# Sparse graph attention on one core: every operation gets a place of its own in its engine's order

## The chip, the cores and the metric

The kernel runs on one NeuronCore of one Trainium2 chip. The metric is the device time of one execution in microseconds (us), measured over several runs; the median is compared. TensorE (PE in the profile), VectorE (DVE), ScalarE (ACT), GpSimd (POOL) and SyncE (SP) each work through a queue of their own, in the order in which the program emits their instructions, and wait for each other by semaphores. SP issues plain transfers; POOL issues the indirect ones (gathers and scatters by a list of row numbers).

## What is computed

One layer of graph attention with a residual, for 16 batches of 1024 nodes with 512 features, 8 heads of 64, all in float32. The adjacency matrix is sparse and shared by all batches; its diagonal is set.

```
h = maximum(layernorm(x), 0)                       # no scale, no offset
q, k, v = h @ Wq + bq, h @ Wk + bk, h @ Wv + bv    # (16, 1024, 8, 64)
scores = einsum('bihd,bjhd->bhij', q, k) / sqrt(64)
scores = scores + where(adj == 0, -1e9, 0)
out = einsum('bhij,bjhd->bihd', softmax(scores), v)
return x + out
```

## The kernel before

**The work.** A score matters only where adj is not 0, so the kernel gathers each node's neighbours and computes nothing dense. It does so in two stages.

The *head* (some 100 us, once) finds the neighbours. SP loads the adjacency as eight tiles of 128 rows (`load_adj`, L664). DVE counts each row's entries (`degree`, L709 and L713), POOL clears the diagonal (`no_diagonal`, L718), `keys` (L724) makes sort keys, TensorE turns them into rows (`flip_row`, L735), and DVE and ACT rank the nodes by comparing (`rank_of`, L745 and L749; `ranks`). Nodes are sorted by degree, so that each tile of 128 nodes needs its own small number of neighbour slots, `CAPS = (11, 8, 6, 5, 4, 3, 3, 2)`. Lists of neighbours are made (`list_of`, L906), scattered to tables in DRAM by POOL (`tell`, `spread`, L910), collected by SP (`collect`, L922), and turned into gather indices (`spots`, `long_rows`, `long_blocks`, `longest`, `pieces`, `slots`). Rows with more than 10 neighbours are cut into *pieces* of 4 that stand in a tile of their own.

The head also projects keys and values of batch 0. Its x tiles are loaded by SP (`load_x`, L786), normed and projected like those of every later batch.

The *batches*: DVE makes the statistics of an x tile (`stats`, `variance`, `shift` L813) with a power on POOL (`power`, L809); ACT norms it (`norm`, L823); TensorE transposes it (`flip`, L830), ACT copies it back (`unflip`, L835), TensorE multiplies it with Wk and Wv (`proj_kv`, L843), ACT or DVE takes the result out of PSUM (`evict_kv`, L861 and L859), and SP stores it as rows of k|v (`store_kv`, L885; in batch 0 POOL by a scatter, L881). The attention of one batch runs beside the projections of the next. It goes by 14 *units*, each of 2 to 4 neighbour slots of one tile: `queries` (TensorE), `gather` (POOL by index, L1093; a node's own row by SP, L1091), `multiply` (L1103) and `score` (L1107) on DVE, `exponent` (ACT, L1111), the weighing of v (`weigh_s` on ACT, L1129, eight small activations each; `weigh_v` on DVE, L1123), sums of the slots (`fold` L1134 on DVE or POOL, `join` L1141, or `add_up` on TensorE, L1157), division by the softmax sum (`scale`, L1198), residual (L1207) and output (`put_out`, L1210, a scatter by POOL). The pieces' unit of tile 0 takes its queries from tile 0's: ACT copies them to SBUF (`copy_q`, L1074), and TensorE spreads them to the pieces with a matmul by the matrix `owner` (L1070); `pass_on` (L1177) returns the pieces' softmax sums.

**The bias.** It is added in PSUM by a matmul of a row of ones (`chosen`) with three bf16 parts of the bias (`project`, L841; `add_bias`, L847, for the very first tile). The parts are made once: `load_b` (L682) loads the three vectors into rows of one tile `rest`, and `round` (ACT, L698 and L700) and `remain` (POOL, L703) take turns on it:

```
def round(j):
    if j < 2:
        nc.scalar.activation(part, rest, AF.Identity, scale=later[j])
    else:
        nc.scalar.copy(bias, rest)
def remain(j):
    nc.gpsimd.tensor_tensor(rest, rest, part, ALU.subtract)
```

**What sets the order.** `planned` (from L265) lists every operation with its engine, what it must follow, which buffers of which pool it uses, and a *place*: a number computed from the batch, the tile or unit, one offset for each kind of operation (`AT`, L73) and some single corrections (`FINE`, L83). `Plan.ordered` (L179 to L257) then plays the program through with a cost for each kind (`LENGTHS`, L106): whenever an engine is free, it takes the operation with the lowest place among those whose inputs are done and whose buffers are free. The sequence that comes out is the order in which the operations are emitted, and so each engine's queue. An operation that is not ready in this play-through is passed by others.

Transfers issued by SP use eight semaphores in turn, so each waits until the eighth before it has landed.

Of the kernel before, what the change touches and what calls it, by code (L numbers as in the profile page):

```python
# [32 lines left out]
P = 128  # L33
H = 8
# [26 lines left out]
LAST_TILES = (0, 1, 2, 3, 4, 5, 6, 7)  # L61
LAST_ORDER = tuple(UNITS.index(unit) for t in LAST_TILES for unit in PARTS[t])
LAST_DIRECT = (7,)
POOL_FOLDS = ((5, 0), (4, 0), (1, 0), (1, 4), (-1, 0))
# [8 lines left out]
AT = dict(  # L73
    load_x=170.09, stats=-5.83, variance=-6.1, power=-47.58, shift=-11.83, norm=-65.99, flip=-3.5, unflip=-69.44, proj_kv=-0.17,
    evict_kv=-1.04, queries=-0.21, own=7.45, gather=-8.51, score=1.54, exponent=37.66, row_sums=-33.29, share=-103.18,
    weigh_v=-4.42, weigh_s=56.4, fold=-4.42, join=-3.58, add_up=-5.47, direct_residual=3.86, direct_out=-0, more=-116.77,
    pass_on=-0.94, sums=-5.02, scale=-1.48, residual=-38.62, put_out=-47.81, seen=11.6, zero=-5.59, zero_rate=0.56,
    ahead=-14.69, early=0.02, early2=0.33, early3=0.24, first=-60.83, first_rate=7.61, v_late=9.54, key_row=-221.51,
    rank_row=-80.11, rank_d=-9.75, rank_a=45.47, ranks=-75.78, ends=-96.51, list_of=76.9, tell=-79.58, spread=-44.68,
    others=-101.81, spots=-59.47, long_rows=-152.98, long_0=-64.75, long=-72.37, longest=20.9, count=-6.64, pieces=2.43,  # L80
    setup=-64.27, parts=-10.1, spread_bias=-5.47, copy_q=131.7, fetch_q=-35.12, evict_v=0.78, bias_v=-48.9,
)
FINE = {  # L83
    ('owners',): -1.5, ('rank_of', 0): 5.46, (-1, 'evict_kv', 7, 0): 0.78, (-1, 'proj_kv', 2, 1): 6.9,
    (-1, 'proj_kv', 6, 0): 9.56, (-1, 'proj_kv', 7, 0): 8.02, (0, 'multiply', 4): 10.01, (0, 'queries', 0, 1): -1.48,
    (0, 'queries', 0, 7): 5, (0, 'weigh_s', 5, 0): -10.62, (1, 'evict_kv', 3, 1): -0.64, (1, 'flip', 1): 0.71,
    (1, 'fold', 11, 1, 1): 0.79, (1, 'fold', 12, 2, 2): 2.15, (1, 'fold', 8, 1, 1): 1.26, (1, 'fold', 8, 2, 2): 2.12,
    (1, 'gather', 8, 3): 0.98, (1, 'join', 9): 3.14, (1, 'multiply', 5): 1.61, (1, 'multiply', 6): 1.34,
    (1, 'proj_kv', 0, 0): -0.95, (1, 'proj_kv', 2, 0): 1.26, (1, 'put_out', 0, 4): -1.57, (1, 'put_out', 0, 5): -2.25,
    (1, 'score', 13): -5.29, (1, 'score', 5): 3.73, (1, 'score', 9): -0.38, (1, 'shift', 1): 3.92, (1, 'weigh_s', 6, 1): 1.85,  # L90
    (1, 'weigh_v', 11): -2.61, (1, 'weigh_v', 9): -1.9, (2, 'add_up', 1): 3.15, (2, 'add_up', 3): 6.42,
    (2, 'evict_kv', 5, 1): 3.83, (2, 'gather', 12, 0): 1.34, (2, 'gather', 3, 1): -1.6, (2, 'gather', 4, 2): -1.63,
    (2, 'gather', 6, 2): -2.75, (2, 'gather', 7, 2): -2.05, (2, 'gather', 8, 3): -1.07, (2, 'gather', 9, 0): 2.03,
    (2, 'gather', 9, 1): 2.13, (2, 'proj_kv', 1, 1): 1.06, (2, 'proj_kv', 2, 1): 1.64, (2, 'proj_kv', 3, 0): 14.3,
    (2, 'proj_kv', 4, 1): -0.54, (2, 'proj_kv', 6, 0): -1.82, (2, 'residual', 0, 4): 2.64, (2, 'residual', 0, 6): 7.2,
    (2, 'score', 7): -2.13, (2, 'store_kv', 6): -3.35, (2, 'variance', 1): 1.8,
# [3 lines left out]
JOIN = False  # L100
BIAS_V = {0: 'DVE', 2: 'DVE', 4: 'DVE', 6: 'DVE'}
PAIRED = ()
FETCH = False


LENGTHS = dict(  # L106
    zeros=(0.15, 2.0, 0.0), load_w=(0.2, 2.5, 3.0), load_b=(0.6, 2.2, 0.0), load_adj=(0.2, 2.5, 1.5),
    spread_bias=(0.22, 0.2, 0), copy_bias=(0.47, 0.15, 0), bias_v=(1.43, 0.0, 0),
    setup=(1.0, 0.1, 0), add_bias=(0.22, 0.2, 0), join_acc=(0.602, 0.13, 0),
    parts_at=(0.4, 0.13, 0), warm=(1.3, 0.1, 0), round=(0.58, 0.15, 0), remain=(1.2, 0.1, 0), degree=(1.4, 0.13, 0), no_diagonal=(0.3, 0.1, 0),  # L110
    keys=(0.45, 0.13, 0), flip_row=(0.45, 0.2, 0), copy_row=(0.68, 0.13, 0), rank_of=(1.28, 0.13, 0), ranks=(1.1, 0.13, 0),
    ends=(1.1, 0.13, 0), list_of=(2.46, 0.13, 0), tell=(1.28, 2.5, 0), spread=(1.5, 2.5, 0), collect=(0.05, 2.6, 0),
    others=(1.25, 0.13, 0), perm_of=(0.4, 0.13, 0), spots=(4.0, 0.13, 0), long_rows=(1.25, 4.0, 1.5), long_blocks=(3.4, 0.13, 0),
    longest=(1.02, 0.13, 0), count_pieces=(0.8, 0.13, 0), first_piece=(0.45, 0.2, 0), owners=(0.95, 0.13, 0), flip_owners=(0.27, 0.2, 0),
    copy_owners=(0.25, 0.13, 0), list_pieces=(0.4, 0.2, 0), pieces=(1.0, 0.13, 0), slots=(1.6, 0.13, 0),
    load_x=(1.25, 3.0, 0.68), stats=(0.818, 0.13, 0), variance=(0.1, 0.13, 0), power=(1.2, 0.0, 0), shift=(0.08, 0.13, 0),
    norm=(0.719, 0.13, 0), flip=(0.437, 0.2, 0), unflip=(0.465, 0.15, 0), proj_kv=(3.649, 0.2, 0), evict_kv=(0.465, 0.15, 0),
    store_kv=(0.1, 2.6, 1.36), proj_q=(3.649, 0.2, 0), evict_q=(0.465, 0.15, 0), store_q=(0.1, 2.6, 0.68), fetch_q=(1.25, 3.0, 0.68),
    queries=(3.649, 0.2, 0), copy_q=(0.487, 0.15, 0), gather=(1.25, 3.0, 1.36), multiply=(0, 0.13, 0), score=(0, 0.13, 0),
    exponent=(0.125, 0.14, 0), row_sums=(0.371, 0.13, 0), share=(0.117, 0.13, 0), weigh_v=(0, 0.13, 0), weigh_s=(1.91, 0.14, 0),  # L120
    fold=(0, 0.13, 0), join=(0.602, 0.13, 0), add_up=(0.858, 0.2, 0), more=(0.133, 0.13, 0), pass_on=(0.14, 0.2, 0),
    scale=(0.602, 0.13, 0), residual=(0.602, 0.13, 0), put_out=(1.30, 3.0, 0.68), seen=(0.25, 0.13, 0),
)
LENGTHS["fold", "POOL"] = LENGTHS["residual", "POOL"] = (1.43, 0.0, 0)
LENGTHS["evict_kv", "DVE"] = (0.602, 0.13, 0)
LENGTHS["gather", "SP"] = (0.1, 3.0, 1.36)
LENGTHS["load_x", "SP"] = (0.2, 2.5, 0.75)
LENGTHS["store_kv", "POOL"] = (1.25, 2.6, 1.36)
PAIR = {1: 0.602, 2: 1.131, 3: 1.668, 4: 2.198}
SHARED = ("fold", "join", "bias_v",  "weigh_v", "residual", "scale", "power")  # L130


BY_UNIT = ("gather", "multiply", "score", "exponent", "weigh_v", "weigh_s", "fold", "join", "add_up", "share")
BY_TILE = ("load_x", "stats", "norm", "flip", "unflip", "proj_kv", "evict_kv", "store_kv", "bias_v")
BY_HOME = ("queries", "row_sums", "residual", "put_out", "scale", "more", "pass_on", "copy_q", "store_q", "fetch_q", "seen")


def spot_of(key, B):

    name, *rest = key
    if name in BY_UNIT:
        b, at = divmod(rest[0], NU)
    elif name in BY_TILE:
        b, at = divmod(rest[0], NT)
    elif name in ("variance", "power", "shift"):
        b, at = divmod(rest[0], NT // group_of(rest[0] * GROUP)[2])
    elif name in BY_HOME:
        b, at = rest[0], 0  # L150
    else:
        return (name, *rest)
    return (min(b, 1) + (b == B - 1), name, at, *rest[1:])


class Plan:

# [6 lines left out]
    def add(self, key, engine, place, after=(), uses=(), length=None, delay=None, moves=None):  # L170

        self.number[key] = len(self.ops)
        long, late, bytes_ = LENGTHS.get((key[0], engine)) or LENGTHS[key[0]]
        length = long if length is None else length
        delay = late if delay is None else delay
        place = place + FINE.get(spot_of(key, self.batches), 0.0)
        self.ops.append((key, engine, length, place, after, uses, delay, bytes_ if moves is None else moves))

    def ordered(self, bufs):  # L179
        ops = [op[:3] + (round(op[3], 4),) + op[4:] for op in self.ops]  # L180
        follow = [[] for _ in ops]
        missing = [len(op[4]) for op in ops]
        left, line = {}, {}
        for i, op in enumerate(ops):
            for key in op[4]:
                follow[self.number[key]].append(i)
        for op in sorted(ops, key=lambda op: op[3]):
            for use in op[5]:
                if use not in left:
                    left[use] = 0  # L190
                    line.setdefault(use[0], []).append(use)
                left[use] += 1
        given = {pool: 0 for pool in line}
        has = set()

        def can_start(op):
            for use in op[5]:
                if use not in has:
                    pool = use[0]
                    n = given[pool]  # L200
                    if line[pool][n] != use or (n >= bufs[pool] and left[line[pool][n - bufs[pool]]]):
                        return False
# [1206 lines left out]
```

## Time and profile before

| what | value |
| --- | --- |
| timed runs | 1636.62, 1629.81 and 1636.53 us, median 1636.53 us |
| profiled execution | 1644.55 us, span 1642.9 us |
| mean granted TensorE clock | 0.989 of full speed |
| instructions | 19494 |
| DMA | 531.71 MB, 324 GB/s over the span |
| first multiply (L1103) of batch 0 | 108.58 us |
| last projection of K and V ends | 1534.0 us |

The profile is one execution, taken by the hardware profiler; its span is the time between its first and last instruction. The page lists the busy time of each engine with the number of instructions, then the span in slices. Other answers of the trace: the same busy times for any stretch (with the TensorE clock that was granted, the busy share of the DMA engines and their GB/s), the waits of an engine (what ended each, the sum, how many, the longest), and a timeline (start, length, engine, line, output <- input, shape, how many instructions in a row, and in brackets the idle time before them with what ended it). A name with q at the end, as SPq, is that engine's issuing of transfers. Two TensorE records belong to one float32 matmul of 128x512.

### The profile page before, as it was taken

What the parts mean: (1) busy time and instruction counts of PE and PEld (TensorE: products, weight loads), DVE (VectorE), ACT (ScalarE), POOL (GpSimd) and SP (SyncE); (2) the same over time, 40 slices, a digit from 0 to 9 for tenths busy, and PEclk for the clock granted to TensorE, in tenths of its full rate; (3) what the DMA queues carried; (4) which work ended last, traced back from release to release, by engine and by line L of the source; (5) the groups of instructions that cost most, each with busy time, mean ns of one, the idle gap of its engine ahead of it and who ended that gap; (6) DMA issues with size and microseconds to landing.
All of it is one profiled execution on the core that took longest, in us unless ns stands there. A gap on an engine that the chain in (4) does not pass through costs nothing. (4 is left out here: it accounts for less than half of the span.)

```text
span 1642.9 us, 19494 instructions
## 1 busy us (share of the span) xinstructions
PE 1574.6 (96%) x4236; PEld 729.9 (44%) x4236; DVE 1525.6 (93%) x2081; ACT 1444.9 (88%) x5420; POOL 1248.7 (76%) x1184
## 2 busy tenths in 40 slices
PE   6899999999999999999999999999999999999696
PEld 3454444444444444444444444444444444444232
DVE  7779999999999999999999999999999999999996
ACT  4258989998998989899898999989999998999885
POOL 3766878778878877887878877888787778777764
PEclk9999999999999999999999999999999999999898
DMA  6487989989899998989999998999989899998993
GB/s 246 138 313 242 360 328 338 362 318 365 313 347 329 355 355 318 358 318 349 336 331 365 327 370 302 337 337 348 352 322 349 301 346 336 348 354 312 339 359 123
DMA packets 150740, 531.71 MB, mean 324 GB/s; under 512 B 19916, under 2 KB 19916, under 8 KB 150616
## 3 DMA queue, kind: packets, MB, share of 16 engines
q0 software_dynamic: 109840, 390.70, 66.6%
q1 hardware_dynamic: 40776, 139.71, 22.0%
q14 instruction: 89, 0.73, 0.1%
q8 instruction: 35, 0.57, 0.1%
HBM read 429.51 MB, written 100.82 MB: 323 GB/s over the span
## 5 line engine op out<-in xcount | busy, mean ns | idle before, releaser
L1129 ACT ACTIVATE g<-g,weights 128x64 f32<-128x64 f32 x4696 | 1154.4, 337 | 18.8 <-DVE weights L1116 10.8
L1093 POOL DMA_INDIRECT g<-kv,index x608 | 638.9, 1051 | 221.7 <-issue 176.4
L843 PE MATMUL pq<-wq,hT 128*128 128x512 f32 x1024 | 460.3, 592 | 0.0
L843 PE MATMUL pk<-wk,hT 128*128 128x512 f32 x960 | 432.9, 594 | 0.0
L843 PE MATMUL pv<-wv,hT 128*128 128x512 f32 x960 | 431.5, 592 | 0.1
L1107 DVE TENSOR_REDUCE weights<-g 128x32 f32<-128x2048 f32 (+2 forms) x224 | 422.5, 1888 | 0.7
L1103 DVE TENSOR_TENSOR g<-g,pq 128x1536 f32<-128x1536 f32 (+2 forms) x208 | 388.7, 1870 | 27.5 <-DMA g<-kv,index 11.3
L843 PEld LDWEIGHTS pq<-wq,hT 128*128 128x128 f32 x1024 | 194.6, 190 | 221.5 <-issue 217.8
L843 PEld LDWEIGHTS pk<-wk,hT 128*128 128x128 f32 x960 | 182.9, 191 | 216.9 <-issue 212.9
L843 PEld LDWEIGHTS pv<-wv,hT 128*128 128x128 f32 x960 | 180.1, 190 | 191.6 <-issue 187.6
L1134 DVE TENSOR_TENSOR g<-g 128x512 f32<-128x512 f32 (+1 forms) x301 | 253.5, 844 | 8.1 <-ACT g L1129 5.3
L1210 POOL DMA_INDIRECT out_dram<-x,perm x128 | 137.8, 1076 | 40.8 <-issue 18.9
L788 POOL DMA_INDIRECT x<-in_x_dram,perm x128 | 131.7, 1029 | 38.5 <-issue 37.6
L1134 POOL TENSOR_TENSOR g<-g 128x512 f32<-128x512 f32 x90 | 114.0, 1275 | 5.0 <-DVE g L1134 2.8
L1111 ACT ACTIVATE weights<-weights 128x32 f32<-128x32 f32 (+2 forms) x224 | 49.8, 223 | 77.2 <-DVE weights L1107 60.5
L1123 DVE TENSOR_TENSOR g<-g,weights 128x512 f32<-128x512 f32 x149 | 109.0, 739 | 2.9 <-ACT weights L1111 2.8
L1207 POOL TENSOR_TENSOR x<-x,o 128x512 f32<-128x512 f32 x67 | 86.1, 1285 | 17.8 <-DVE o L1198 14.9
L823 ACT ACTIVATE h<-x,shift,rstd 128x512 f32<-128x512 f32 x120 | 92.4, 806 | 0.5 <-DVE shift L813 0.5
L830 PEld LDWEIGHTS pht<-ident,h 128*128 128x128 f32 x512 | 64.3, 145 | 63.6 <-issue 54.2
L1157 PE MATMUL acc<-g,ident 128*128 128x512 f32 x170 | 83.9, 607 | 2.4 <-ACT g L1129 1.5
L835 ACT COPY hT<-pht 128x512 f32<-128x512 f32 x128 | 73.0, 575 | 14.9 <-PE pht L830 13.1
L797 DVE BATCH_NORM_STATS2 st<-x 128x6 f32<-128x512 f32 x120 | 81.5, 679 | 2.5 <-DMA x<-in_x_dram,perm 2.4
(242 smaller groups left out, 1108.3 us busy)
## 6 DMA issues: line engine op xcount, KB each, us to landing
g<-kv SPq DMA_DIRECT2D x128, 512.0 KB
kv<-kvt SPq DMA_DIRECT2D x120, 512.0 KB
g<-kv,index POOLq DMA_INDIRECT x608
adj<-in_adj_dram SPq DMA_DIRECT2D x8, 512.0 KB
x_first<-in_x_dram SPq DMA_DIRECT2D x8, 256.0 KB
x<-in_x_dram,perm POOLq DMA_INDIRECT x128
out_dram<-x,perm POOLq DMA_INDIRECT x128
wk<-in_L_gnn_Wk_dram SPq DMA_DIRECT2D x1, 1024.0 KB
```

The lines of the kernel that those rows point to most:

```text
L788: nc.gpsimd.indirect_dma_start(out=X[n][:], out_offset=None, in_=x_rows, in_offset=on(ap=perm[:, t : t + 1], axis=0), element_offset=b * N * D
L823: nc.scalar.activation(HN[n], X[n], AF.Relu, bias=shift, scale=scale)
L843: nc.tensor.matmul(pt, HT[n][:, c, :], W[name][:, c, :], start=(apart and c == 0), stop=(n != -NT and c == DC - 1))
L1093: nc.gpsimd.indirect_dma_start(out=G[i][:, s].rearrange("p j d -> p (j d)"), out_offset=None, in_=KV[b % len(KV)][:], in_offset=on(ap=inde ...
L1103: nc.vector.tensor_tensor(k, k, Q[b, t][:, None, :].to_broadcast([P, count, D]), ALU.mult)
L1107: nc.vector.tensor_reduce(weights[:, w, :], heads(G[i][:, :count, 0, :]), AX.X, ALU.add)
L1123: nc.vector.tensor_tensor(v, v, own.to_broadcast([P, n, H, HD]), ALU.mult)
L1129: nc.scalar.activation(v[:, h, :], v[:, h, :], AF.Identity, scale=weights[:, c + s, h : h + 1])
L1134: engine.tensor_tensor(v[:, 0:n], v[:, 0:n], v[:, first : first + n], ALU.add)
L1157: nc.tensor.matmul(ACC[b, home], owner_t if t < 0 else ident, v[:, s, :], start=(u == added_up(b, B, home)[0] and s == 0), stop=(u == adde ...
L1207: (nc.vector if residual_by_vector(b, B, t) else nc.gpsimd).tensor_tensor(rows, rows, add, ALU.add)
L1210: nc.gpsimd.indirect_dma_start(out=out_rows, out_offset=on(ap=perm[:, t : t + 1], axis=0), in_=X.pop(b * NT + TILES.index(t))[:], in_offse ...
```

## The change

The set of operations stays the same, but for three small matmuls that are added, a dependence that is replaced, and two tiny copies that vanish with a path that was switched off.

1. **Order.** The offsets, corrections, costs and the play-through go. In their place a table `PLACES` gives every operation a number of its own: one block for operations that happen once, one for the projections of batch 0 (`first`), one each for batches 0, 1 and 2, one for the batches 3 to 13, one for batch 14 (`next`) and one for batch 15 (`last`). A batch's numbers are moved by `PERIOD` for each batch. `ordered` sorts each engine's operations by this number alone, so an operation is never passed by another of its engine; the queues are merged so that everything is emitted behind what it needs.
2. **Dependences.** `round(0)` must now follow the second norm instead of the first power.
3. **TensorE warmed.** `warm_pe`: three float32 matmuls of 128x512 on the tile that the biases go into, their results unused. They are first in TensorE's queue.
4. **Last batch.** The order of its units is written out as a list: unit 6 now comes ahead of 9, and unit 3 ahead of 5.
5. **Dead code.** Fetching the pieces' queries from DRAM, joining the pieces on DVE, and a column of `found0` go, with two one-column copies of DVE (L998 and L1019). A multiplication on POOL (`weigh_p`) is added, but no unit uses it.

The diff, cut to its core (the other changes of `planned` take the place and the costs out of each `add`):

```diff
-AT = dict(
-    load_x=170.09, stats=-5.83, variance=-6.1, power=-47.58, shift=-11.83, norm=-65.99, flip=-3.5, unflip=-69.44, proj_kv=-0.17,
...
+PERIOD = 95.290021
+PLACES = {
+    'once': dict(
+        zeros=(9.38,),
+        load_w=(2.39, 6.93, 22.86,),
+        load_b=(13.19, 1.37, 6.73,),
+        load_adj=(1.87, 3.6, 4.6, 2.13, 3.77, -0.33, 3.93, 1.93,),
+        warm=(89.31,),
+        warm_pe=(3.75,),
+        setup=(-0.4, 0.06, 3.61,),
+        parts_at=(10.69,),
+        round=(4.36, 4.39, 6.59,),
+        remain=(2.93, 16.84,),
+        degree=(10.86, 14.18, 21.61, 11.08, 14.91, 10.62, 17.65, 12.88,),
...
+    'first': dict(
+        load_x=(94.59, 95.26, 95.84, 97.13, 101.65, 101.71, 104.87, 110.73,),
...
+        power=(95.83, 104.16, 131.48, 140.22,),
...
     def ordered(self):
+        place = self.places()
+        number = self.number
+        known = [[number[key] for key in op[2]] for op in self.ops]
+        waiting = {}
+        for i in sorted(range(len(self.ops)), key=place.__getitem__):
+            waiting.setdefault(self.ops[i][1], []).append(i)
...
+        while len(result) < len(self.ops):
+            ready = []
+            for engine, queue in waiting.items():
+                if head[engine] == len(queue):
                     continue
...
+                i = queue[head[engine]]
+                new = [use for use in self.ops[i][3] if use not in has]
+                if all(k in made for k in known[i]) and all(given[use[0]] == at[use] for use in new):
+                    ready.append((place[i], i, new))
+            _, i, new = min(ready)
...
+    add(("warm_pe",), "PE")
...
-        known = [("remain", j - 1)] if j else [("parts_at",), ("power", -NT // 2)] + [("load_b", name) for name in names]
-        add(("round", j), "ACT", AT["parts"] + j, known)
+        known = [("remain", j - 1)] if j else [("parts_at",), ("norm", 1 - NT)] + [("load_b", name) for name in names]
+        add(("round", j), "ACT", known)
...
-LAST_TILES = (0, 1, 2, 3, 4, 5, 6, 7)
-LAST_ORDER = tuple(UNITS.index(unit) for t in LAST_TILES for unit in PARTS[t])
+LAST_ORDER = (10, 11, 12, 13, 8, 6, 9, 7, 4, 3, 5, 2, 1, 0)
...
+        def warm_pe():
+            p = ps_a.tile([P, D], F32, tag="acc", name="p_warm")
+            for _ in range(3):
+                nc.tensor.matmul(p, ident, rest, start=True, stop=True)
```

(`first` numbers are lowered by one `PERIOD`, so they stand on the same scale as `once`; the three entries of `load_b` are those of k, v and q.)

## The prediction

> **What bounds the kernel now.** I read the page's busy line first, then the same sums by stretch, then TensorE's waits, then the timeline of the first 27 us. The busy line:
>
> ```profile
> span 1642.9 us, 19494 instructions
> ...
> PE 1574.6 (96%) x4236; PEld 729.9 (44%) x4236; DVE 1525.6 (93%) x2081; ACT 1444.9 (88%) x5420; POOL 1248.7 (76%) x1184
> ```
>
> TensorE leads, but a mean over stages does not say where it waits. By stretches (start:end, length, then busy us of each engine with its instructions, granted clock, DMA share, GB/s):
>
> ```profile
> 0.00:40.00 40.00, 26.65 (x84) 13.90 (x85) 29.67 (x83) 18.92 (x30) 14.12 (x35) 1.00 0.71 253
> ...
> 200.00:1440.00 1240.00, 1226.10 (x3302) 568.20 (x3301) 1180.42 (x1513) 1151.47 (x4368) 987.38 (x917) 1.00 0.93 339
> 1440.00:1534.00 94.00, 94.00 (x249) 43.14 (x247) 88.79 (x111) 86.79 (x334) 72.10 (x68) 1.00 0.93 344
> 1534.00:1605.00 71.00, 53.37 (x119) 22.21 (x118) 63.72 (x61) 63.70 (x267) 45.14 (x44) 0.88 0.92 337
> ```
>
> In the long middle TensorE idles 1240 - 1226.1 = 13.9 us and nobody else comes near; from 1534 on (no projections left) DVE and ACT lead, and the serial output transfers end the run. So a change of order can gain at most about 14 us in the middle, and something at the two ends. TensorE's own waits (us in all, times, longest):
>
> ```profile
> PE pht_first L830 <- ACT h_first L823: 11.2, 1, 11.2
> ...
> PE pht L830 <- ACT h L823: 6.2, 1, 6.2
> ...
> PE pq_-1_10415 L1070 <- ACT q L1074: 2.2, 1, 2.2
> PE p_key L735 <- DVE key L724: 1.7, 1, 1.7
> ```
>
> The third is the repeated one: the pieces' query (L1070) waits for ScalarE's copy of tile 0's query (L1074) in nearly every batch. The timeline of the middle gives these waits as .48, .06, .96, 1.13, .1, 1.05, .1, 1.22, .05, .9, 2.19, 1.33 and 1.39: 11.0 us together. Another 2.4 us are short waits for free PSUM at L841.
>
> **The head, +7 us (bounds 0 and +16).** Every operation of the first 100 us gets a new place. The one that matters is the load of the K bias. All three bias vectors (6 KB each, as three equal rows) go into one tile, which round(0) (L698) reads, and round(0) is now queued on ACT behind the second norm. Before, the three loads are SP's 4th to 6th transfers, issued at 2.19 to 2.95 us, and the round runs at 9.71:
>
> ```profile
> 9.71 0.72 ACT L698 ACTIVATE scratch<-scratch,later 128x512 bf16<-128x512 f32 x1 [7.22 <-DMA scratch<-in_L_gnn_bq_dram]
> ```
>
> After, SP's order is four x tiles with one adjacency tile and bv among them, three more adjacency tiles, wk (10th), the other four, two x tiles, bq (17th), wv (18th), the seven zero stores (19th to 25th), an x tile, and only then bk, the **27th**. SP issues a transfer only when the eighth before it has landed (the program's instruction list shows that wait on each). Before, its last transfers of the same stretch go out so:
>
> ```profile
> 20.95 3.21 SPq L676 DMA_DIRECT2D told<-scratch  x2
> 24.43 0.94 SPq L676 DMA_DIRECT2D lists<-scratch  x2
> 25.98 0.33 SPq L786 DMA_DIRECT2D x_first<-in_x_dram  x1
> ```
>
> The 25th is issued at about 25, the 27th at 25.98. After, as many bytes lie ahead, so bk is issued at about 25.5 and lands at about 27.5 (25.5 to 29).
>
> What queues behind: on POOL remain(0) stands fourth, ahead of one setup and of power for the second pair of tiles; behind that power stands DVE's shift, and behind the shift five of the eight degrees (L709, L713) and the keys. From the rows: round 0.72, remain 1.16 with a start of 0.05, setup 0.7, power 0.73, shift 0.2: DVE is free at 31.1. Five degrees at 1.35 make 37.9, the keys 0.46: 38.3, where TensorE now gets them here:
>
> ```profile
> 24.25 1.09 PE L735 MATMUL p_key<-ident,key 128*128 128x128 f32 x8 [1.69 <-DVE key L724]
> ```
>
> That is 14 us later. TensorE meanwhile: three warming matmuls as soon as bv is there (about 8.3), two sets of flips to 13.5, the first K projection when wk has landed behind 4 MB (15.7 at 2.6 us for a MB, the 383 GB/s of 12 to 24 us) until 19.2, then a wait of about 12.8 us for the next norm (31.9, the same POOL queue), flips, the bias matmul at 33.6, one projection to about 39. At the end of the rank flips it stands 49.5 against 37.6, with 18.3 us of work done against 22.0: 15.6 us behind.
>
> What takes part of it back: in the profiled run TensorE stands idle 6.23 us from 77.24, for norms that ACT (9.05 us idle) and DVE (4.62) deliver only after 81.14, and then works at half clock until 87, another 1.8 us:
>
> ```profile
> 77.00:80.00 3.00, 0.23 (x1) 0.00 (x0) 0.00 (x0) 0.00 (x0) 1.32 (x2) 1.00 0.77 209
> 80.00:81.00 1.00, 0.00 (x0) 0.00 (x0) 0.00 (x0) 0.00 (x0) 0.00 (x0) 0.58 0.41 164
> 81.00:87.00 6.00, 3.53 (x11) 2.72 (x12) 5.14 (x31) 5.56 (x10) 3.85 (x4) 0.50 0.46 147
> ```
>
> A TensorE that is 15.6 us behind still has projections to do there, so these 8.0 us go: 15.6 - 8.0 = +7.6. DVE's chain, 14 us later at the long rows, has 13.7 us of idle pieces between 60 and 108.6 us, where the first multiply (L1103) stands, to catch up in: about 1 us late. By this path the first multiply comes at about 115.5, +7. I take +7. The lower end, 0, is a bk that lands as early as bq does; the upper, +16, is TensorE's whole lag with no stall to swallow it.
>
> The three added matmuls (L899 to L902 of the changed file): eight such records take 3.60 us at L843, six take 2.7, or 5.4 at half clock. They lie where TensorE has nothing else, before the first norm. Bounds: -2.2 (the first flips took 1.97 against 1.04 us later, the first projection 4.83 against 3.60) and +2.7; I take 0, since the wait for the second norm comes behind them and ends later than either.
>
> Here a rule bears. By the rows above, the granted clock stays at 1.00 for some 3 us of idling and then falls to half; a 12.8 us wait at 19.2 must cool it again, and I have put 1.7 us of slow work behind it. The Trainium skill, TensorE: Matmul & The Clock Gate, Part 1, says that the clock falls back after an idle window of about 3.4 us. By that page the warming would be lost as well, and the waits of 1 to 2 us in the middle would never cool the clock, so that 1.7 us of the next part would drop out of the sum.
>
> **The middle, -12.7 us (bounds -15 and 0).** The pieces' query now stands five TensorE operations (12 us of work) behind tile 0's query instead of two (7.3 us), while the copy keeps its place on ACT to within one or two operations; the longest wait of 2.19 us is less than the 4.7 us gained. So 11.0 us go. The longest wait also cost clock, 3.4 us at half speed, 1.7 us lost:
>
> ```profile
> 1236.00:1238.00 2.00, 1.49 (x3) 0.73 (x4) 2.00 (x5) 1.97 (x8) 1.66 (x2) 0.82 0.45 182
> 1238.00:1240.00 2.00, 2.00 (x4) 0.88 (x3) 2.00 (x2) 2.00 (x6) 1.70 (x2) 0.50 0.73 125
> ```
>
> 11.0 + 1.7 = 12.7. Next late on TensorE is nothing long: its work of one batch is about 95.1 us, DVE's 91, ACT's 89, and the 14 periods from one pass_on to the next average 96.2. At the other end, a reordered ACT or POOL queue makes a new wait of the same size, and the gain is 0. The two tiny copies that vanish (0.3 us of DVE) lie beside idle time: nothing.
>
> **The tail, -3 us (bounds -7 and +4).** Behind the last projection the chain is DVE and ACT work, then output transfers one after another (3.75 us each from 1617 to 1637.63). The last batch's pieces' query, which waits 4.0 us today, stands four projections before the end of the last K and V instead of two (7.3 us of work), so its units can start earlier; the last unit must still wait for the stored rows and its gathers, some 13 us behind the last projection. I take less than half of 7. The order of the last units also changes (unit 6 now ahead of 9, unit 3 ahead of 5): nearly the same work, so +4, one output, is the other end.
>
> **Sum.** +7 - 12.7 - 3 = -8.7 on the profiled execution's 1644.55: 1635.85. The median of the timed runs, 1636.53, is 0.9951 of the profiled one, so 1627.8. Half a per cent (1628.4 to 1644.7 around the median), about what a measurement of this kernel can tell, is just reached.
>
> **Rivals.**
> - *No stall to swallow the lag.* The timed runs lie 8 us under the profiled one; if that is the stall at 77 us, the head costs 15: +15 - 12.7 - 3 = -0.7, 1643.85, scaled 1635.8. For it: the size fits. Against: the engines stop there for data that any run must fetch.
> - *The late bias sets the pace and the middle gains nothing.* One mechanism: bk as 27th transfer holds POOL, DVE and TensorE until 31; TensorE, which has 96% of the span to work, never gets its 15.6 us back, and the pieces' query finds another late operand. It decides once bk lands after about 23 us, when the keys pass the 24.25 of today by more than the 8.0 of the stall. +15.6 - 3 = +12.6: 1657.15, scaled 1649.0. For it: TensorE has no slack later. Against: the copy's distance grows by more than its longest wait.
> - *The bias comes early after all* (SP not held by the eight transfers): head 0, -15.7: 1628.85, scaled 1620.9. Against: the issue times 13.21 to 25.98 of SP's queue.
>
> **Chances.** Forecast 0.50 (0.33 of it past the half per cent, 0.17 within); no stall to swallow 0.13, within; late bias without gain 0.25, slower; early bias 0.12, faster. Faster 0.45, same 0.30, slower 0.25. The range goes from the low ends together (0 - 15 - 7: 1614.6) to a little past the slower rival, 1615 to 1652; that rival's own high end with +4 in the tail lies outside.
>
> **What would show it.** In the changed profile: the first round (L915) with an idle time before it that ends on bk at about 27.5; TensorE idle some 12 us before its second flips; the first key flips at about 39; the first multiply (L1307) at about 115; no waits of 1 us and more at the pieces' query (L1284) and a period near 95.2; a last projection's end some 6 us earlier. If the round runs before 12 us the head is wrong; if TensorE's idle time between 200 and 1440 is still above 10 us the middle is.

## The result

The changed kernel takes **1657.15 us** (median of 4 runs, 1651.62 to 1658.57) against 1636.57 us (1629.81 to 1636.78): ratio 1.013, interval 1.0095 to 1.0164. Measured again on another chip it took 1654.51 against 1634.2, ratio 1.0139 (1.011 to 1.0169). It is slower by 20 us, where 9 us less were forecast, and the range (1615 to 1652) does not hold it.

### The profile page after: what moved, and what is told of

It reads as the page before. It is cut to its first block, busy times and chain, and to the rows that moved or that the text cites. A ratio compares the mean times of both kernels' runs of the same rounds, so it can differ in the third digit from the quotient of the medians.

```text
span 1649.9 us, 19575 instructions
## 1 busy us (share of the span) xinstructions
PE 1577.1 (96%) x4242; PEld 728.0 (44%) x4242; DVE 1543.9 (94%) x2079; ACT 1441.9 (87%) x5420; POOL 1254.9 (76%) x1184
## 5 line engine op out<-in xcount | busy, mean ns | idle before, releaser
L1297 POOL DMA_INDIRECT g<-kv,index x608 | 628.4, 1034 | 203.5 <-issue 165.3
L1307 DVE TENSOR_TENSOR g<-g,pq 128x2048 f32<-128x2048 f32 (+2 forms) x208 | 388.5, 1869 | 27.0 <-DMA g<-kv 12.3
L1413 POOL DMA_INDIRECT out_dram<-x,perm x128 | 147.5, 1152 | 50.6 <-issue 30.9
L1327 DVE TENSOR_TENSOR g<-g,weights 128x512 f32<-128x512 f32 x149 | 121.6, 825 | 1.6 <-ACT weights L1315 1.5
L1040 ACT ACTIVATE h<-x,shift,rstd 128x512 f32<-128x512 f32 x120 | 96.6, 808 | 3.8 <-DVE shift L1030 2.7
```

Of the source, the lines that this page charges most:

```text
L1040: nc.scalar.activation(HN[n], X[n], AF.Relu, bias=shift, scale=scale)
L1297: nc.gpsimd.indirect_dma_start(out=G[i][:, s].rearrange("p j d -> p (j d)"), out_offset=None, in_=KV[b % len(KV)][:], in_offset=on(ap=inde ...
L1307: nc.vector.tensor_tensor(k, k, Q[b, t][:, None, :].to_broadcast([P, count, D]), ALU.mult)
L1327: nc.vector.tensor_tensor(v, v, own.to_broadcast([P, n, H, HD]), ALU.mult)
L1413: nc.gpsimd.indirect_dma_start(out=out_rows, out_offset=on(ap=perm[:, t : t + 1], axis=0), in_=X.pop(b * NT + TILES.index(t))[:], in_offse ...
```

## The profile after

The profiled execution took 1651.62 us, the shortest of the four; that of before, 1644.55, was longer than every timed run. So the two traces show only 7 of the 20 us. The page:

```profile
span 1649.9 us, 19575 instructions
...
PE 1577.1 (96%) x4242; PEld 728.0 (44%) x4242; DVE 1543.9 (94%) x2079; ACT 1441.9 (87%) x5420; POOL 1254.9 (76%) x1184
```

By stretches (columns as in the prediction's table of stretches):

```profile
0.00:40.00 40.00, 18.70 (x50) 9.36 (x51) 19.24 (x59) 9.76 (x15) 7.90 (x27) 0.83 0.67 239
...
200.00:1440.00 1240.00, 1227.14 (x3307) 566.86 (x3306) 1200.16 (x1517) 1150.32 (x4376) 990.75 (x918) 1.00 0.94 339
1440.00:1534.00 94.00, 93.67 (x247) 42.53 (x246) 88.36 (x107) 84.66 (x325) 70.21 (x66) 1.00 0.93 337
1534.00:1605.00 71.00, 53.98 (x120) 22.39 (x120) 67.10 (x61) 65.26 (x271) 48.29 (x44) 0.88 0.90 329
```

In the first 40 us TensorE is busy 18.70 us instead of 26.65, 5.1 of them warming. The middle is hardly changed: idle 12.9 us instead of 13.9, so the prediction's own sign that its middle is wrong (above 10) is there. TensorE's waits:

```profile
PE pht_first L1047 <- ACT h_first L1040: 12.5, 1, 12.5
PE acc L1365 <- issue: 9.3, 4, 8.3
PE pq L1058 <- DVE g L1307: 7.5, 13, 1.1
...
PE pk L1058 <- ACT kvt L1078: 4.5, 5, 1.7
...
PE pq_-1_13020 L1284 <- ACT q L1288: 1.9, 1, 1.9
```

The pieces' query waits for its copy in the last batch alone. In its place stands a wait of about half a microsecond in nearly every batch, for a query's PSUM buffer that a multiply on DVE (L1307) still reads. The head, on ACT (an instruction a row: start, length, engine, line, what, and in brackets the idle time before it with what ended it):

```profile
26.19 0.72 ACT L915 ACTIVATE scratch<-scratch,later 128x512 bf16<-128x512 f32 x1 [13.05 <-DMA scratch<-in_L_gnn_bk_dram]
```

and on TensorE:

```profile
6.94 5.13 PE L902 MATMUL p_warm<-scratch,ident 128*128 128x512 f32 x6 [6.94 <-DMA scratch<-in_L_gnn_bv_dram]
11.92 1.04 PE L1047 MATMUL pht_first<-ident,h_first 128*128 128x128 f32 x8
...
30.64 1.12 PE L1047 MATMUL pht_first<-ident,h_first 128*128 128x128 f32 x4 [12.54 <-ACT h_first L1040]
...
37.93 1.04 PE L952 MATMUL p_key<-ident,key 128*128 128x128 f32 x8
```

The K bias is issued at 23.93 us and the round starts on it at 26.19; the second flips come at 30.64, the keys' at 37.93.

## The experiments

The theories that the expectations name:
- **T1**: three terms: the late K bias costs the head 9 to 15 us, the new order gains some 6 to 10 in the batches 5 to 13, its tail loses 4 to 6.
- **T2**: the order of the batches costs the time, and the head's lag is swallowed on the way (as the forecast had it for half of the lag).
- **T3**: the new order makes TensorE's signals arrive late (see the last section).
- **T4 to T6** are local rivals, told where they are tested.

All kernels but the plainest are made from the changed one. In the mixes, `places()` gives way to a table of ranks: an operation has its rank in the sequence of the old or of the new order, according to its batch, so that inside each part every engine's order is exactly the old or the new one.

```diff
-        place = self.places()
+        place = RANK
```

### The old order through the new code: h0_all_old

All ranks old, old dependence of the first round, old last batch, no warming.

> Every operation in the order of the kernel before, emitted by the new code from a table of ranks; dependence, last batch and missing warming as before. Only the two one-column copies of DVE are gone. T1 and T3: within 0.5% of the kernel before. Its profile is a second look at the old order: whether TensorE's idle time at 77 us and its late signals are there again.

1634.84 us against 1634.2: ratio 1.0001 (0.9981 to 1.0022). So the new code by itself, the dead code and the two copies cost and gain nothing: the time lies in the order, with the dependence and the warming that this kernel leaves out. Its trace decided one of the forecast's terms. The same stretches in which TensorE stood still in the first profile:

```profile
72.00:77.00 5.00, 5.00 (x19) 2.71 (x18) 4.38 (x29) 3.64 (x6) 3.78 (x5) 1.00 0.77 242
77.00:80.00 3.00, 2.95 (x14) 1.82 (x14) 2.76 (x15) 2.24 (x5) 2.39 (x3) 1.00 0.75 243
80.00:81.00 1.00, 1.00 (x4) 0.51 (x3) 0.93 (x4) 0.74 (x2) 0.70 (x2) 1.00 0.76 209
81.00:87.00 6.00, 6.00 (x23) 3.13 (x22) 4.16 (x12) 3.45 (x6) 4.60 (x5) 1.00 0.76 245
```

TensorE is busy throughout, at full clock. So the 6.23 us of idling and the 1.8 us of slow clock are no part of the old order. A wait of 9 to 10 us at the same place of the head stands in four of the 19 traces: the first profile of before and the three traces taken on the first chip (e1, e2, h2). The last section returns to it. Without it the old order's first multiply comes at 100.91 us, and the changed kernel's 12.6 us later:

```profile
100.91 1.21 DVE L1519 TENSOR_TENSOR g<-g,pq 128x1024 f32<-128x1024 f32 x1
```

```profile
113.47 1.21 DVE L1307 TENSOR_TENSOR g<-g,pq 128x1024 f32<-128x1024 f32 x1
```

### The whole change again: r_after

> The changed kernel again, to stand beside the others on one chip. T1 (late K bias in the head, +15, middle -6, tail +4): 13 to 20 us over the kernel before. T3 (the new order of the batches lets TensorE's signals arrive late, batch after batch, as in the profile of the early-bias kernel, where eleven of ACT's waits for finished matmuls take 40 us): 40 to 60 us over it on a chip where that happens, with the excess spread over the batches 3 to 13.

1654.51 against 1634.2. Between its trace and that of h0_all_old, on the same chip, the time can be laid out by a marker: the issue of the last K and V store of each batch by SP. Microseconds behind h0_all_old:

```
                      batch 1   batch 6   batch 14   batch 15   end of span
changed kernel           9.0      16.4       4.8        7.5        13.2
r_after                  9.9      18.1       7.1        8.5        13.0
e1b_bias_early          -3.4       6.9       0.1        3.4         7.0
e1c_bias_early          -5.4       2.4      -4.8       -1.7         2.0
h4_old_once              0.5       8.9      -0.7        1.6         6.1
k2_outputs               0.3       5.8      -3.4       -1.0        -0.5
before, first profile    7.6       9.1       5.0        5.0         6.1
```

Along a row one reads: up to batch 1 the late head costs 9 to 10; from batch 1 to 6 another 6 to 10 are lost, in every kernel with the new order of the batches, most of it by the stores of batch 4; the batches 7 to 14 give back 7 to 12 (of which 4 are h0_all_old's own, since the row of before gains them too); from there to the end 6 to 8 are lost again (2.9 in k2). T1 holds in kind, with a term that it lacked.

### The bias early: e1, e1b, e1c

```diff
-        load_b=(13.19, 1.37, 6.73,),
+        load_b=(1.36, 1.37, 1.38,),
```

> The changed kernel with one edit: the K and Q biases are loaded beside the V bias, as SP's 5th to 7th transfers, instead of 27th and 17th. Theory T1 (the late K bias costs the time): the first round runs at about 9 us instead of 26.2, the keys' flips at about 25 instead of 37.9, and the kernel takes some 14 us less than the changed one's 1657, about 1643. Theory T2 (the new order of the batches costs the time and the head's lag is swallowed on the way): the head shows the same early round, but the time stays within 1653 to 1657.

> The changed kernel with all three biases loaded early, once more, beside others on one chip. T1 (the late bias costs the head 9 to 10 us by the end of batch 0's projections, as the second look at the old order against the changed one shows): that much under the changed kernel, 8 to 12 us over the kernel before. T3 (late signals of TensorE's finished matmuls belong to this program): again 50 us over it, with waits of 3 to 10 us before ACT's copies in the batches 4 to 10. If they belong to the chip of that run, they are gone.

> The early-bias kernel once more, as the base of the one with the outputs: 8 to 12 us over the kernel before.

On the first chip 1696.04 against 1645.37 (the last section returns to it); on the second 1645.01 against 1633.35 (1.0074, 1.0046 to 1.0101), on the third 1641.69 against 1634.46 (1.0042, 1.0024 to 1.006). So the change costs 12 and 7 us with it, instead of 20, where T1 had 8 to 12. The edit moves the load of the Q bias too, which was issued at 12.11 us, some 12 us ahead of K's. The head of e1b on ACT and TensorE:

```profile
13.79 0.72 ACT L915 ACTIVATE scratch<-scratch,later 128x512 bf16<-128x512 f32 x1
```

```profile
24.41 1.09 PE L952 MATMUL p_key<-ident,key 128*128 128x128 f32 x8 [0.54 <-DVE key L941]
```

The round runs at 13.79 without a wait for a DMA (not at 9 as expected, since it stands behind the second norm on ACT), and the keys come at 24.41, as in the old order. At batch 1 (the table of markers) e1b and e1c are 12 to 15 us ahead of the changed kernel. **The one late load of 6 KB is worth 9 to 13 us of the 20.** T2 falls.

### Without the warming: e2_no_warm

```diff
-    add(("warm_pe",), "PE")
```

> The changed kernel without the three warming matmuls. T1: TensorE stands idle where they were, and the first flips and the first projection take 2.2 us more, at half clock, before the same wait for the second norm: within 1 us of the changed kernel's 1657. T2 says the same. A third theory, that the warming delays the first projection, expects 2 to 5 us less.

1704.95, on the first chip, 9 us above e1_bias_early there: the bias's share, as far as a chip with large other delays can tell; for the warming itself the time is inconclusive. Its trace shows what warming buys: the first flips take 1.97 us instead of 1.04 and the first projection 6.49 instead of 3.67, ahead of the same wait. The second flips then come at 30.86 and the keys at 38.84 us, 0.2 and 0.9 us behind the changed kernel's, so in the head the warming costs nothing and gains little.

### Mixes of old and new order: h2, h1b, h3, h5, h6, h4

The tables of ranks are cut so: h2 has the new order ahead of batch 5 and the old one from there; h1b the reverse; h3 the new order to batch 13 and the old one in the last two; h5 the old order to batch 2 and h6 to batch 7, the new one behind; h4 the old order only in the head (loads, biases, degrees) and in the projections of batch 0. A first cut with the seam at batch 5 (h1) has no time: in it the engines' queues wait for each other in a circle.

> The opposite mix: head and batches 0 to 4 in the order of the changed kernel (without the warming), batches 5 to 15 in the order of the kernel before. T1: the whole head lag and no gain behind it, 1657 to 1660. T2: near the kernel before, 1637 to 1643.

> Head and batches 0 to 4 in the order of the kernel before (no warming), batches 5 to 15 in the new order. T1: -6 in the middle and +4 in the tail, about 2 us under the kernel before. T3: 25 to 45 us over it, if late signals cost the new order as much on this chip as in the earlier profiles.

> The changed kernel with the batches 14 and 15 alone in the order of the kernel before. T1: the tail's 4 us come back, so 4 us under the changed kernel of the same chip. T3: no more than that either, since the batches 3 to 13 keep the new order.

> Head and batches 0 to 2 in the old order, batches 3 to 15 in the new one. T1: also the 7 us that the new order loses in the batches 0 to 2 are gone; -10 in the middle, +6 in the tail and the seam remain: from 4 us under the kernel before to 10 over it. T4 (the new order's middle is not better at all): 6 over it or more, with periods behind the seam of 96 and above.

> Head and batches 0 to 7 in the old order, batches 8 to 15 in the new one. T1: half of the middle's gain, -4, +6 in the tail, and the seam: 2 to 15 us over the kernel before. The period falls from about 96 to 95.5 us at the seam.

Measured, against before on the same chip: h2 1690.68 (1645.37), h1b 1667.14 (1634.2), h3 1678.04 (1634.2), h5 1662.67 (1633.35), h6 1668.7 (1633.35). All miss T1's numbers, because the seam itself costs 13 to 30 us by the marker of the table. The time from one pass_on (L1380 in the changed kernel) to the next, which is near 96 elsewhere (in the new order's first three batches 103, 102 and 87), is 117.31 and 109.48 us in h1b at its seam, 105.69 and 117.32 in h3, 110.41, 104.66 and 100.12 in h5, 117.43 and 109.81 in h6. These two orders can't be joined in the middle without loss. The likely reason, not traced, is that an operation that one queue has early stands behind work that the other queues have late. So the mixes don't decide between T1 and T4: the periods behind the seam, up to batch 13, average 95.9 us in h1b and 96.0 in h6, but 96.4 in h5, and the old order's own are 96.36 in the first profile.

> Head and projections of batch 0 in the order of the kernel before (no warming), all attention and the batches 1 to 15 in the new order. T1: the head's 9 to 10 us are gone and the rest of the change stays, so about the same as with the early bias, 3 to 10 us over the kernel before, plus what the seam between the orders costs.

With the seam in the head there is no such loss: 1645.13 against 1633.35 (1.0075, 1.0047 to 1.0104), as predicted by T1 and equal to the early bias. Two ways of taking the late bias away end in the same place.

### What the wait for the copy is worth: k1, k5, k6

The old order throughout; in the batches 1 to 14 (k5 and k6: 1 to 13) ACT's queue is changed in one place, here for k1 and k5:

```diff
-weigh_s(u9, 1) weigh_s(u9, 2) evict_kv(j6, k) copy_q
+weigh_s(u9, 1) copy_q weigh_s(u9, 2) evict_kv(j6, k)
...
-weigh_s(u9, 1) weigh_s(u9, 2) evict_kv(j6, k) copy_q
+weigh_s(u9, 1) evict_kv(j6, k) copy_q weigh_s(u9, 2)
```

> The order of the kernel before throughout, with one kind of move: in the batches 1 to 14 ACT copies tile 0's query one weighing (8 small activations, 1.9 us) earlier. The prediction's step of the middle says that TensorE's waits for this copy cost 11 us in all: they vanish from its list of waits, and the kernel takes 8 to 11 us less than the kernel before. T5 (the waits only move: DVE at 95% or the projections' own operands stop TensorE next): the waits vanish, and the time falls by 0 to 4 us.

> The order of the kernel before, with ACT's eviction and the copy of tile 0's query behind it both one weighing (1.9 us) earlier in the batches 1 to 13. With the copy alone moved, TensorE's waits went over to the eviction, 11.4 us in 17 waits. If what was missing is ACT's time at this place, both waits fall and the kernel takes 4 to 9 us less than the kernel before; if a wait turns up elsewhere again, 0 to 3 us.

> The same with both of them two weighings earlier (3.8 us). If the place on ACT decides, the same gain or one more microsecond; if DVE's folds behind the delayed weighings become late, less than with one weighing.

k1: 1632.48 against 1634.46, ratio 0.9984 (0.9966 to 1.0002). The waits for the copy are gone from batch 1 on but for one of 0.3 us, and TensorE's list of waits has this in their place:

```profile
PE pk L1270 <- ACT kvt L1290: 11.4, 17, 1.3
...
PE pq_-1_13024 L1496 <- ACT q L1500: 5.2, 1, 5.2
```

(The second line is the last batch, not touched.) The eviction stands behind the same weighing as before, and now behind the copy too; TensorE, no longer held by the copy, waits for it instead, 11.4 us where the old order's two traces have 4.0 and 2.3. **11 us of waits taken away, 7 to 9 come back at the next buffer**, T5. k5, which moves both, takes 1630.33 against 1633.04, ratio 0.9985 (0.9972 to 0.9997), a gain of 2.7 us; its list still has 6.7 us of waits for the eviction. k6, with both 3.8 us earlier, takes 1650.22 (1.01, 1.008 to 1.012): 14 waits of up to 1.2 us for the eviction and 11 of up to 1.9 us for the norm, about one of each in a batch.

### The outputs of the tail: k2_outputs

The early-bias kernel with three outputs earlier on POOL:

```diff
-        put_out=(134.28, 138.23, 146.81, 174.73, 181.64, 220.25, 226.43, 264.65,),
+        put_out=(134.28, 138.23, 146.81, 174.73, 181.64, 220.25, 226.43, 229.85,),
...
-        put_out=(197.43, 189.43, 177.33, 183.91, 174.2, 167.76, 162.77, 147.96,),
+        put_out=(197.43, 189.43, 177.33, 183.91, 174.2, 167.76, 150.05, 141.9,),
```

> The early-bias kernel with three outputs earlier in POOL's queue: the last of batch 14 behind two gathers instead of behind the third output of batch 15, the first two of batch 15 right behind their residuals. T1 (the tail loses its time to nine outputs in a row, 3.6 us each, where the old order has four): the end comes 4 to 6 us earlier than in the early-bias kernel of this call. T6 (the tail is late because DVE and ACT finish late): no more than 1 us.

1638.81 against e1c's 1641.69 on the same chip, 2.9 us less. What was wrong in the changed kernel's tail shows on POOL:

```profile
1616.34 1.00 POOL L1413 DMA_INDIRECT out_dram<-x,perm  x1 [0.60 <-issue]
...
1622.42 1.19 POOL L1413 DMA_INDIRECT out_dram<-x,perm  x1 [1.19 <-issue]
1625.63 0.96 POOL L1413 DMA_INDIRECT out_dram<-x,perm  x1 [2.02 <-DMA out_dram<-x,perm]
...
1629.09 0.98 POOL L1413 DMA_INDIRECT out_dram<-x,perm  x1 [1.21 <-issue]
...
1632.58 1.01 POOL L1413 DMA_INDIRECT out_dram<-x,perm  x1 [1.20 <-issue]
...
1636.10 1.04 POOL L1413 DMA_INDIRECT out_dram<-x,perm  x1 [1.21 <-issue]
...
1639.85 0.99 POOL L1413 DMA_INDIRECT out_dram<-x,perm  x1 [1.42 <-DMA out_dram<-x,perm]
...
1644.00 0.98 POOL L1413 DMA_INDIRECT out_dram<-x,perm  x1 [1.87 <-DMA out_dram<-x,perm]
```

Seven outputs one behind the other, each 3.2 to 4.2 us after the last. Three of the rows name the landing of the output ahead as what they waited for; the others have the same spacing, and an output lands 3.0 us (median) after its issue. Before, there were four:

```profile
1626.18 1.47 POOL L1210 DMA_INDIRECT out_dram<-x,perm  x1 [0.28 <-POOL x L1207]
...
1630.12 0.98 POOL L1210 DMA_INDIRECT out_dram<-x,perm  x1 [1.02 <-issue]
...
1633.89 0.98 POOL L1210 DMA_INDIRECT out_dram<-x,perm  x1 [0.28 <-POOL x L1207]
1637.63 0.96 POOL L1210 DMA_INDIRECT out_dram<-x,perm  x1 [2.76 <-DMA out_dram<-x,perm]
```

The second of the seven belongs to batch 14: the new order puts it behind three outputs of batch 15. In k2 five stand in a row, and the last one waits for DVE:

```profile
1622.47 0.98 POOL L1413 DMA_INDIRECT out_dram<-x,perm  x1 [1.23 <-DMA out_dram<-x,perm]
1626.18 0.97 POOL L1413 DMA_INDIRECT out_dram<-x,perm  x1 [1.43 <-issue]
1630.68 0.98 POOL L1413 DMA_INDIRECT out_dram<-x,perm  x1 [2.24 <-DVEq L1582]
```

T1 is right about the place, and high by a factor of about 1.7 in the price. In the table of markers, k2 loses 0.5 us behind batch 15, e1c 3.7.

### Cures together: k4_early_head

The new head with early biases and warming, all batches old with k1's earlier copies.

> The new order's head with the early biases and the warming (batch 0's projections end 3.4 us earlier with it than in the old order, by the profiles), all batches in the old order with the earlier copies. T1: 3 us under the kernel with the earlier copies alone; T5: with the copies worth nothing, 3 us under the kernel before. The seam between the orders can cost either.

1634.08 against 1634.46 (0.9997, 0.9982 to 1.0012), 1.6 us above k1: the head's 3 us do not arrive (its first multiply comes at 105.24 us, k1's at 101.40). The best version found is k5_both_early, the old order with two operations of ACT moved, and its lead over the kernel before is 0.15%.

## Why the prediction was wrong

**Right: the chain of the late bias.** Issue at 25.5 (23.93), round at 27.5 (26.19), second flips at 31.9 (30.64), key flips at 39 (37.93), a TensorE wait of 12.8 (12.54), first multiply at 115.5 (113.5). The place of one 6 KB load, read off SP's queue, gave all of these within 2 us. The lag of TensorE at the end of the rank flips was 10 us (47.7 against 37.6), not the 12 that their times gave, and as one projection fewer (3.6 us) was done by then, 14, not 15.6. That the first multiply fits is partly luck: against the first profile it is 5 us late, of the 7 forecast; against the old order without its stall it is 12.6.

**Wrong, first: "a TensorE that is 15.6 us behind still has projections to do there, so these 8.0 us go".** There was nothing to swallow the lag: the stall at 77 us is not in the second trace of the old order, and the timed runs, 8 us below the profiled one, had hinted at it. The forecast took a wait of ACT that the profile explains by no instruction ("remote") in one execution for part of the program, and its reason against the first rival, that the engines stop there for data that any run must fetch, isn't in the rows: ACT and DVE stood before operations whose inputs TensorE and DVE themselves had made. The first rival had this mechanism and the price, 15; it measured 9 to 13. The second rival, a late bias and no gain in the middle (+12.6), was nearest as a whole; what it lacked is a tail that loses. That its unscaled 1657.15 is the measured median to the digit is chance: it stands on the scale of the profiled execution.

**Wrong, second: the middle, "so 11.0 us go".** The waits for the copy did go, as forecast. But the term priced a wait at its length. In the new order TensorE waits instead for query buffers, 7.5 us in 13 waits, and in k1 for the eviction, 11.4 us in 17; taking the copy's waits away from the old order brought 2.0 and 2.7 us. ACT, at 93% in the middle, is late by as much as before, and TensorE meets that at the next thing it needs from ACT or DVE. What the new order as a whole gains in the batches 5 to 13 is 0.2 to 1.1 us a batch (periods of 95.65 to 96.2 us against 96.36 and 96.79 in the old order's two traces), 1 to 10 us in all, if it is a gain at all (h5). From batch 1 to 6 it **loses 6 to 10 us**, which no step had: the batches 0 to 2 have blocks of `PLACES` of their own, and the forecast priced one pattern for all. That these blocks are the cause is not shown; h5, meant to show it, drowned in its seam. TensorE's waits there are short ones, 9.6 us in e1b_bias_early between 100 and 580 us (longest 2.4) against 6.3 in h0_all_old, which explains only a part. Together the term of -12.7, from batch 1 to 14, measured -4.2 and -2.8 in the changed kernel's two traces against h0_all_old, and between -3.7 and +3.5 in the others of the table with the new order.

**Wrong, third: the tail, -3.** The pieces' query of the last batch did come earlier against its need (wait 1.9 instead of 4.0), but the end hangs on outputs that wait for each other. The forecast saw this chain at 3.75 us each (true from 1626 us on; the output at 1617 lies 9 us ahead of it) and looked at the order of the units, not of the outputs; batch 14's last output had moved into the middle of batch 15's. It cost +4 to +6, of which 2.9 came back by moving three outputs.

**Sum of the measured terms**, against h0_all_old's trace: 9.9 for the head, 8.2 for the batches 1 to 6, -11.0 to batch 14, 5.9 behind it: 13.0 in the pair of traces. The medians differ by 20.3. The rest is a spread between executions: the trace of r_after (1651.42) is its shortest run, 3.1 us under the median, and that of h0_all_old (1638.43) lies 4.2 us above the median of before. Which terms would carry these 7 us, no pair of traces settles.

**The clock.** The Trainium skill, TensorE: Matmul & The Clock Gate, Part 1, lets the clock fall after an idle window of about 3.4 us, free-running. After the 12.54 us wait the clock was at half until about 35.5 us, as both the page and the row had it. For short waits the traces differ from the page, and they decide: an idle time of 2.42 us in e1b_bias_early at 491 us,

```profile
491.00:493.00 2.00, 0.24 (x1) 0.00 (x0) 1.93 (x6) 2.00 (x10) 1.01 (x1) 1.00 1.00 399
493.00:495.00 2.00, 1.34 (x2) 0.65 (x3) 2.00 (x4) 1.14 (x6) 1.09 (x2) 0.60 1.03 418
495.00:497.00 2.00, 2.00 (x4) 0.89 (x3) 2.00 (x3) 1.90 (x4) 1.57 (x2) 0.54 1.01 373
```

brought it to half; one of 2.05 us in h0_all_old at 844 us took it to 0.50, and one of 2.40 us there before 1330 left it at 1.00. So in these runs a wait of 2 us can cost clock, and doesn't always.

## What to carry to other kernels

A wait in a profile is worth its length only if nobody else is as late: before taking it as a gain, ask which engine was late, and where the same lateness is met next. When every operation has a fixed place, look at the smallest transfers first: one 6 KB load 27th in SP's queue held POOL, and behind it DVE and TensorE, for 14 us. A stall whose releaser the profile does not name, in an execution that is longer than the timed runs, belongs in no sum before a second trace shows it.

## What was not expected of the hardware

**Engines can stand still for microseconds with no recorded reason, and where they did again and again, the same program took 3% longer.** In the first profile of the kernel before, TensorE's projection of L843 ends at 72.7 us (69.11 + 3.60), and ACT, idle, takes its result out only here:

```profile
71.28 0.81 ACT L823 ACTIVATE h<-x,after_told 128x512 f32<-128x512 f32 x1 [0.81 <-DMA x<-in_x_dram,perm]
81.14 0.58 ACT L861 COPY kvt_first<-pv_first 128x512 f32<-128x512 f32 x1 [9.05 <-remote]
```

"Remote" is written where no recorded instruction explains the release. DVE stands still until the same moment, ahead of an operation that reads only what DVE itself wrote 4.6 us earlier:

```profile
75.93 0.59 DVE L939 COPY spot<-after_lists 128x8 f32<-128x8 f32 x7
81.14 0.18 DVE L1035 TENSOR_SCALAR index<-spot 128x38 int32<-128x38 f32 x1 [4.62 <-remote]
```

So a late signal of TensorE, as T3 has it, isn't all that happens there. In h0_all_old the same copy comes 0.57 us after ACT is free, at 73.24. In e1_bias_early on the first chip the stall of the head (9.7 us, until 82 us) is there as well, and ten more such waits of ACT between 570 and 1380 us (ACT's waits: in all, how many, longest):

```profile
ACT hT L1052 <- remote: 27.5, 7, 9.7
...
ACT kvt L1078 <- remote: 12.4, 4, 4.1
```

and the same kernel on two other chips had none, and took 51 and 54 us less, while the kernel before differed by 11 to 12 us between those chips. So T3 falls as a property of the order alone; that the new order suffers more where it happens is what the runs of that one chip suggest (against before: e1 1.03, 1.0257 to 1.0342; e2 1.0335, 1.0289 to 1.0381; h2 1.0268, 1.0225 to 1.0311), but the changed kernel itself wasn't run there. What holds the engines stays open.

**The same DVE operation takes up to three times as long while POOL runs an operation with two inputs.** In 480 to 1440 us, the multiplication of v (L1123 before, L1327 after; the number before the last bar is its mean in ns):

```profile
L1123 DVE TENSOR_TENSOR g<-g,weights 128x512 f32<-128x512 f32 x89 | 67.2, 764 | 0.0
```

```profile
L1327 DVE TENSOR_TENSOR g<-g,weights 128x512 f32<-128x512 f32 x91 | 76.4, 849 | 0.3 <-ACT weights L1315 0.3
```

Taken one by one, the mean splits in two. Of before's 89, 84 meet no two-input operation (TENSOR_TENSOR) of POOL and take 682 ns on average; the 5 that do take 2149. Of the changed kernel's 91, 72 meet none and take 679; the 19 that do take 1492. No operation without such a neighbour took more than 739 ns. In the changed kernel two of DVE's take 2.78 us beside one of POOL's, where one alone takes 0.68:

```profile
482.80 2.78 DVE L1327 TENSOR_TENSOR g<-g,weights 128x512 f32<-128x512 f32 x2
495.83 0.68 DVE L1327 TENSOR_TENSOR g<-g,weights 128x512 f32<-128x512 f32 x1
```

```profile
483.74 1.28 POOL L1346 TENSOR_TENSOR g<-g 128x512 f32<-128x512 f32 x1
```

The old scheduler kept the two-operand operations of DVE and POOL apart (its list `SHARED`); the new table does not, and DVE is busy 931.0 instead of 913.3 us of these 960, 9.2 of the difference at this line. What this adds to the kernel's time wasn't tried.
